# Attention row sums: 15 of 24 steps folded by GpSimd and reduced by VectorE instead of accumulated by ScalarE

## The chip, the cores and the metric

The kernel runs on one core of one Trainium2 chip. The metric is the device time of one execution in microseconds. Before the change it is 11398.82 us, the median of three runs (11398.53 to 11410.69). The profiled execution has a span of 11403.8 us with a mean granted TensorE clock of 0.894.

## What is computed

The reference is a network of four layers on an input of 4 images, 128 channels, 64 by 64. Only the attention of layer 2 is touched. Each image is 4096 tokens with 128 features, that is 16 heads of 8. Queries, keys and values are one and the same matrix:

```python
q = jnp.transpose(qkv, (0, 2, 1, 3))
scores = jnp.einsum('bhsd,bhtd->bhst', q, q) / np.sqrt(D)
attn = jax.nn.softmax(scores, axis=-1)
ctx = jnp.einsum('bhst,bhtd->bhsd', attn, q)
```

As queries and keys are equal, the score matrix is symmetric: a block of exps and its transpose serve both halves. The softmax is taken without a maximum, as exps divided by their sums at the end. A sum for a token has two sources: one from the product of the exps with a column of ones, and one, for transposed blocks, from the row sums of the exps. It is the row sums that the change moves.

## The kernel before

The layer works on one image at a time. For each of the four images `attention` runs once (line 909), between stages that prepare the next image and finish the last. It takes the 16 heads one after another.

**Steps.** The 4096 tokens are four blocks j of 1024 query columns and 16 pairs m of key tiles (256 rows). Because of the symmetry a block j takes only the pairs m from 4j on. Its four own pairs (m // 4 == j) are the diagonal; the later ones are called `behind` and are used twice, straight and transposed. `pairs` (line 962) mixes them: for j=0 three behind and then one own, for j=1 two and one, for j=2 one and one, for j=3 only own. That makes 40 steps for a head, 24 of them behind; steps are counted here from 0 in each head. In order of m they are 4 5 6 0 7 8 9 1 10 11 12 2 13 14 15 3 for j=0 (steps 0 to 15), 8 9 4 10 11 5 12 13 6 14 15 7 for j=1 (16 to 27), 12 8 13 9 14 10 15 11 for j=2 (28 to 35), and 12 to 15 for j=3 (36 to 39).

**What a step does.** TensorE computes scores for two tiles (lines 1082 to 1089) into a ring of three PSUM tiles. ScalarE takes the exps (line 1094), one 128x1024 ACTIVATE for each of the two tiles; in a behind step it also asks for the row sum by `accum_out`, which shows in the trace as an ACTIVATION_READ_ACCUMULATOR after the ACTIVATE. VectorE transposes the exps of behind steps in 32 by 32 blocks (line 1098). One step later `weigh` (line 1026) has TensorE multiply the exps with the values into `ctx_ps`.

**Turns.** The transposed exps of four behind pairs are a group. `turn` (line 980) multiplies one eighth of a group with the spread values `turned_v` into `acc_ps`. After the eighth turn of a group VectorE copies or adds the result into `acc` (lines 1006 and 1008). `turns` (line 1015) does none to three turns in a step and begins a group only two steps after its last transpose. At the end of a block j, `weigh` adds the matching `acc` by the `place` products and VectorE copies `ctx_ps` out (line 1057). TensorE can't start the next block's products before that copy.

**Order.** TensorE follows the source (`manual_schedule` for PE, line 1207): in each step scores, then turns, then the products of the step before. The other engines' order is made by a scheduler when the program is built, and each engine then works through its own in sequence.

**Loads.** `load` (line 921) fetches the keys and queries of a head by 32 small DMAs into a buffer `raw`, and GpSimd rounds `raw` into the fp32r tiles (line 940). `load_values` (line 944) fetches values by four DMAs and has GpSimd spread them by a mask into `turned_v` (line 954).

Of the kernel before, what the change touches and what calls it, by code (L numbers as in the profile page):

```python
# [9 lines left out]
F32 = mybir.dt.float32  # L10
F32R = mybir.dt.float32r
I32 = mybir.dt.int32
AF = mybir.ActivationFunctionType
ALU = mybir.AluOpType
AX = mybir.AxisListType
PSUM = bass.MemoryType.PSUM

P = 128
NB = 4
HW = 64  # L20
L = HW * HW
CH = 512
# [752 lines left out]
def layer2_attention(K, xd, dpool, w):  # L775

    nc, tc, mm = K.nc, K.tc, K.mm
    NH, HD = 16, 8
    NJ = 4
    BT = NTT // NJ  # L780
    scale = 1.0 / math.sqrt(HD)
    with ExitStack() as ctx:
# [126 lines left out]
        def attention(qt, dsum, big, work, pssc, psctx, psacc):  # L909
# [8 lines left out]
            dacc = big.tile([P, NJ - 1, NH, NTT], F32, name="dacc")  # L918
            nc.gpsimd.memset(dacc, 0.0)

            def load(h, queues=(nc.sync, nc.sync)):

                out = []
                for keys in (True, False):
                    t = work.tile([P, L // 2], F32R, name="keys" if keys else "queries")
                    raw = work.tile([P, L // 2], F32, name="raw")
                    n = P if keys else CH
                    for p in range(2):  # L930
                        for c in range(2):
                            for k in range(4):
                                r = unit(p, c).start + HD * k
                                src = head_d[k // 2 if keys else k % 2, HD * h : HD * h + HD]
                                at = p if keys else c
                                queues[not keys].dma_start(
                                    out=raw[r : r + HD].rearrange("d (m s) -> d m s", s=n),
                                    in_=src.rearrange("d (m z s) -> d m z s", z=2, s=n)[:, :, at],
                                )
                    nc.gpsimd.tensor_copy(t, raw)  # L940
                    out.append(t)
                return out

            def load_values(h, j):


                v = work.tile([P, 4 * BT, HD], F32, name="v")
                for a in range(4):
                    nc.sync.dma_start(
                        out=v[32 * a : 32 * a + 32],  # L950
                        in_=value_d[h, :, j].rearrange("s q t d -> s (q t) d"),
                    )
                t = work.tile([P, 4 * BT, 4, HD], F32, name="turned_v")
                nc.gpsimd.tensor_tensor(  # L954
                    t,
                    v.unsqueeze(2).to_broadcast([P, 4 * BT, 4, HD]),
                    quarter.unsqueeze(1).to_broadcast([P, 4 * BT, 4, HD]),
                    ALU.mult,
                )
                return t  # L960

            def pairs(j):

                later = list(range(4 * j + 4, NTT // 2))
                n = len(later) // 4
                for k in range(4):
                    yield from later[n * k : n * k + n]
                    yield 4 * j + k

            steps = [(h, j, m) for h in range(NH) for j in range(NJ) for m in pairs(j)]  # L970
            heads = {0: load(0, (nc.sync, nc.scalar))}
            values = {(0, 0): load_values(0, 0)}
            order = [(h, j) for h in range(NH) for j in range(NJ - 1)]
            cps = psctx.tile([P, CH], F32, name="ctx_ps")
            aps = psacc.tile([P, 2, BT, 32], F32, name="acc_ps")
# [4 lines left out]
            def turn():  # L980

                r, h, j, i, td, _, sums = groups[0]
                if r == 0:
                    sums = groups[0][-1] = aps[:, halves[0] % 2]
                    halves[0] += 1
                groups[0][0] += 1
                tv = values[h, j]
                for g in range(4):
                    n = 4 * r + g
                    q, t = divmod(n, BT)  # L990
                    at = 32 * (4 * t + q)
                    mm(
                        sums[32 * g : 32 * g + 32],
                        tv[:, n].rearrange("p a d -> p (a d)"),
                        td[:, :, at : at + 32],
                        start=r == 0,
                        stop=r == BT - 1,
                    )
                if r < BT - 1:
                    return False  # L1000
                groups.pop(0)
                if i == 1:
                    accs[h] = work.tile([P, NJ - 1, BT, 32], F32, name="acc")
                at = accs[h][:, i - 1]
                if j == 0:
                    nc.vector.tensor_copy(at, sums)  # L1006
                else:
                    nc.vector.tensor_tensor(at, at, sums, ALU.add)
                if i == NJ - 1:
                    after = order.index((h, j)) + 2  # L1010
                    if after < len(order):
                        values[order[after]] = load_values(*order[after])
                return True

            def turns(n, ready):
# [10 lines left out]
            def weigh(h, j, m, exs):  # L1026

                last = m == 4 * j + 3
                first = m == (4 * j + 4 if j < NJ - 1 else 4 * j)
                for p in range(2):  # L1030
                    at = (h * NTT + 2 * m + p) * (HD + 1)
                    for c in range(2):
                        mm(
                            cps[unit(p, c), :],
                            qt[:, at : at + 32],
                            exs[p][:, c, :],
                            start=first,
                            stop=last and j == 0,
                        )
                if not last:  # L1040
                    return
                if j > 0:
                    while any(g[1] == h and g[3] == j for g in groups):
                        turn()
                    for k in range(2):
                        for p in range(2):
                            for c in range(2):
                                a = 2 * p + k
                                mm(
                                    cps[unit(p, c), :].rearrange("r (t a s) -> r t a s", a=4, s=32)[:, :, a],  # L1050
                                    place[:, a, :],
                                    accs[h][:, j - 1, 4 * c : 4 * c + 4],
                                    start=False,
                                    stop=k == 1,
                                )
                u = work.tile([P, CH], F32, name="ctx")
                nc.vector.tensor_copy(u, cps)  # L1057
                for p in range(2):
                    for c in range(2):
                        cols = slice((2 * j + c) * CH, (2 * j + c + 1) * CH)  # L1060
                        r = unit(p, c).start
                        nc.sync.dma_start(out=num_d[p, HD * h : HD * h + HD, cols], in_=u[r : r + HD])
                        nc.sync.dma_start(out=den_d[p, h : h + 1, cols], in_=u[r + HD : r + HD + 1])

            values[order[1]] = load_values(*order[1])


            starts = [n for n, (h, j, m) in enumerate(steps) if m // 4 > j and m % 4 == 0]
# [1 line left out]
            begun = {}  # L1070
            turned = None
            past = None
            for n, (h, j, m) in enumerate(steps):
                keys, queries = heads[h]
                if n == 0 or h != steps[n - 1][0]:
                    if h + 1 < NH:
                        heads[h + 1] = load(h + 1)
                behind = m // 4 > j
                if n in ends:
                    turned = work.tile([P, BT, 2 * CH], F32, name="turned")  # L1080
                    end = min(ends[n], (h + 1) * len(steps) // NH - 2)
                sps = [pssc.tile([P, 2, CH], F32, name="score") for p in range(2)]
                for p in range(2):
                    for c in range(2):
# [2 lines left out]
                            keys[unit(p, c), m * P : (m + 1) * P],  # L1087
                            queries[unit(p, c), j * CH : (j + 1) * CH],
                        )
                exs = []  # L1090
                for p in range(2):
                    ex = work.tile([P, 2, CH], F32, name="ex", bufs=6)
                    t = 2 * m + p
                    nc.scalar.activation(  # L1094
                        ex, sps[p], AF.Exp, scale=scale, accum_out=dacc[:, j, h, t : t + 1] if behind else None
                    )
                    if behind:
                        nc.vector.transpose(turned[:, t % BT, :], ex.rearrange("p c s -> p (c s)"))  # L1098
                    exs.append(ex)
                turns(n, lambda g: begun[id(g[4])] < n - 1)  # L1100
                if past is not None:
                    weigh(*past)
# [4 lines left out]
            while groups:  # L1107
                turn()
            weigh(*past)
            nc.vector.tensor_reduce(dsum, dacc.rearrange("p j h t -> p t h j"), AX.X, ALU.add)  # L1110

        def feed_forward(b, dsum, work, psum):
# [530 lines left out]
```

## Time and profile before

Groups of instructions in the attention, over the whole execution:

| engine, line | what | count | busy us | mean ns |
|---|---|---|---|---|
| ScalarE L1094 | exp, 128x1024 | 5120 | 5015.9 | 1040 |
| ScalarE L1094 | read of the accumulator | 3072 | 680.4 | 221 |
| VectorE L1098 | transpose, 128x1024 | 3072 | 3596.9 | 1219 |
| TensorE L89 | ctx products | 20480 | 2872.8 | 603 |
| TensorE L89 | turns | 24576 | 1750.8 | 387 |
| TensorE L89 | scores | 10240 | 1365.0 | 500 |
| VectorE L1057 | copy of ctx | 256 | 169.7 | 663 |
| GpSimd L954 | spread values, 128x1024 | 192 | 456.4 | 2378 |
| GpSimd L940 | round keys or queries, 128x2048 | 128 | 242.4 | 1894 |

TensorE's matmuls for four parts of the array run beside each other, so their busy times in the table overlap and don't add up to a time. A row's mean is the time of one instruction; the idle time before a group, and what ended it, stand behind it in the page. What sets the pace is read from the order in time.

### The profile page before, as it was taken

How to read it: one execution, taken by the hardware profiler on the slowest of the kernel's cores; microseconds unless marked ns; L12 is line 12 of the kernel's file. 1: busy time of each engine (PE TensorE's matmuls, PEld its weight loads, DVE VectorE, ACT ScalarE, POOL GpSimd, SP SyncE). 2: the span in 40 equal slices, each digit the busy share in tenths (PEclk: the TensorE clock that was granted, in tenths of full speed). 3: DMA queues.
4: the chain of work that ended last, by engine and by line, in shares of the span. 5: the costliest groups of instructions: out<-in, count | busy, mean ns of one | idle time of the engine just before them, and what ended most of it. 6: DMA issues, size and time to landing. Idle time of an engine off the chain costs nothing. (4 is left out here: it accounts for less than half of the span.)

```text
span 11403.8 us, 182690 instructions
## 1 busy us (share of the span) xinstructions
PE 9270.3 (81%) x71376; PEld 3448.3 (30%) x71376; DVE 7274.7 (64%) x7758; ACT 7509.0 (66%) x11610; POOL 2630.9 (23%) x1711
## 2 busy tenths in 40 slices
PE   5777777777759999958999967999967999976766
PEld 2222223222123333323333322333322333323433
DVE  2687687687736666656666655666655666654464
ACT  2564554554428888848888847888846888852331
POOL 0466455565611111121111121111121111110000
PEclk8888878888679999979999979999979999988898
DMA  3322322322122121122211122122122112112103
GB/s 84 89 63 56 95 61 66 86 63 66 49 57 34 32 32 32 34 66 35 37 31 32 24 74 38 32 33 36 24 71 41 31 31 33 31 55 87 49 16 133
DMA packets 524322, 581.50 MB, mean 51 GB/s; under 512 B 106232, under 2 KB 329536, under 8 KB 520896
## 3 DMA queue, kind: packets, MB, share of 16 engines
q1 hardware_dynamic: 520896, 565.61, 21.6%
q8 instruction: 561, 9.19, 0.3%
q10 hardware_dynamic: 2560, 4.20, 0.3%
q14 instruction: 305, 2.50, 0.1%
HBM read 373.96 MB, written 76.55 MB: 40 GB/s over the span
## 5 line engine op out<-in xcount | busy, mean ns | idle before, releaser
L1094 ACT ACTIVATE ex<-score 128x1024 f32<-128x1024 f32 x5120 | 5015.9, 1040 | 665.4 <-PE score L89 657.3
L1098 DVE STREAM_TRANSPOSE turned<-ex 128x1024 f32<-128x1024 f32 x3072 | 3596.9, 1219 | 1595.6 <-ACT ex L1094 1453.1
L89 PE MATMUL ctx_ps<-ex,qt 128*32 128x512 f32 x20480 | 2872.8, 603 | 230.4 <-DVE ctx L1057 229.7
L89 PE MATMUL acc_ps<-turned,turned_v 128*32 128x256 f32 x24576 | 1750.8, 387 | 99.2 <-DVE acc L1006 49.7
L89 PE MATMUL score<-queries,keys 32*128 32x512 f32 x10240 | 1365.0, 500 | 185.4 <-POOL queries L940 182.1
L641 DVE TENSOR_TENSOR_SCAN hs<-decay,carry,hs 128x512 f32<-128x512 f32 x1024 | 1248.0, 1263 | 151.2 <-ACT decay L640 141.9
L640 ACT ACTIVATE decay<-dt,a_neg 128x512 f32<-128x512 f32 x1024 | 699.9, 690 | 883.0 <-DVE hs L641 879.4
L954 POOL TENSOR_TENSOR turned_v<-v,quarter 128x1024 f32<-128x1024 f32 x192 | 456.4, 2378 | 3549.9 <-PE acc_ps L89 3432.7
L89 PEld LDWEIGHTS score<-queries,keys 32*128 32x128 f32 x10240 | 529.3, 183 | 2262.3 <-issue 1589.0
L647 POOL TENSOR_TENSOR hs<-hs,c_sb 128x1024 f32<-128x1024 f32 x512 | 1201.4, 2367 | 49.1 <-DMA c_sb<-c_d 29.4
L89 PEld LDWEIGHTS ctx_ps<-ex,qt 128*32 128x32 f32 x20480 | 683.1, 110 | 832.8 <-DVE ctx L1057 310.3
L89 PEld LDWEIGHTS acc_ps<-turned,turned_v 128*32 128x32 f32 x24576 | 607.3, 108 | 780.2 <-issue 514.9
L89 PE MATMUL y_ps<-hs,pair 128*64 128x512 f32 x2048 | 658.8, 761 | 224.4 <-POOL hs L647 224.3
L637 DVE TENSOR_TENSOR hs<-dtx,b_ps 128x2048 f32<-128x2048 f32 x256 | 581.5, 2271 | 316.8 <-PE b_ps L89 227.8
L1094 ACT ACTIVATION_READ_ACCUMULATOR ex<-score 128x1 f32 x3072 | 680.4, 221 | 0.0
L89 PE MATMUL ln_var<-ln_sq,mean 128*128 128x512 f32 x448 | 296.3, 748 | 220.5 <-ACT ln_sq L104 185.1
L89 PE MATMUL b_ps<-dbc,spread 32*128 32x512 f32 x512 | 343.8, 756 | 149.6 <-DVE hs L637 149.6
L89 PE MATMUL conv<-under,deep 96*32 96x512 f32 x1536 | 283.2, 715 | 74.4 <-DMA under<-xp 54.6
L89 PEld LDWEIGHTS y_ps<-hs,pair 128*64 128x64 f32 x2048 | 138.3, 161 | 674.2 <-POOL hs L647 418.0
L940 POOL CAST keys<-raw 128x2048 fp32r<-128x2048 f32 x64 | 121.1, 1892 | 917.9 <-DMA raw<-head_d 865.2
L644 POOL COPY carry<-hs 128x4 f32<-128x4 f32 x256 | 64.9, 253 | 1108.9 <-DVE hs L641 1096.0
L1057 DVE COPY ctx<-ctx_ps 128x512 f32<-128x512 f32 x256 | 169.7, 663 | 198.5 <-PE ctx_ps L89 198.5
(340 smaller groups left out, 8583.1 us busy)
## 6 DMA issues: line engine op xcount, KB each, us to landing
raw<-head_d SPq DMA_DIRECT2D x1984, 64.0 KB
c_sb<-c_d SPq DMA_DIRECT2D x512, 128.0 KB
dt<-dt SPq DMA_DIRECT2D x128, 256.0 KB
dtx<-dtx SPq DMA_DIRECT2D x128, 256.0 KB
w<-in_L_ffn_weight SPq DMA_DIRECT2D x32, 1024.0 KB
w<-in_L_ffn_weight SPq DMA_DIRECT2D x128, 256.0 KB
under<-xp SPq DMA_DIRECT2D x384, 66.0 KB
under<-fp SPq DMA_DIRECT2D x384, 66.0 KB
```

The lines of the kernel that those rows point to most:

```text
L89: self.nc.tensor.matmul(out, lhsT, rhs, start=start, stop=stop)
L637: nc.vector.tensor_tensor(hs, dtx2, bb.unsqueeze(1).to_broadcast([P, NQ, CH]), ALU.mult)
L640: nc.scalar.activation(ex, dt2[:, q, :], AF.Exp, scale=a_neg[:, q, g : g + 1])
L641: nc.vector.tensor_tensor_scan(hs[:, q, :], ex, hs[:, q, :], carry[:, g, q : q + 1], ALU.mult, ALU.add)
L644: nc.gpsimd.tensor_copy(carry[:, g, :].unsqueeze(2), hs[:, :, CH - 1 : CH])
L647: nc.gpsimd.tensor_tensor(at, at, cs.unsqueeze(1).to_broadcast([P, 2, CH]), ALU.mult)
L940: nc.gpsimd.tensor_copy(t, raw)
L954: nc.gpsimd.tensor_tensor(t, v.unsqueeze(2).to_broadcast([P, 4 * BT, 4, HD]), quarter.unsqueeze(1).to_broadcast([P, 4 * BT, 4, HD]), ALU.mult,
L1057: nc.vector.tensor_copy(u, cps)
L1094: nc.scalar.activation(ex, sps[p], AF.Exp, scale=scale, accum_out=dacc[:, j, h, t : t + 1] if behind else None)
L1098: nc.vector.transpose(turned[:, t % BT, :], ex.rearrange("p c s -> p (c s)"))
```

## The change

Of the 24 behind steps of a head, 15 no longer ask ScalarE for the row sum. `folded` names them: for j=0 m = 4, 5, 7, 8, 10, 11, 13, 14; for j=1 m = 8, 10, 12, 14; for j=2 m = 12, 13, 14. For these GpSimd adds the two halves of each tile's exps (128x1024 out) and then the halves of that (128x512 out), and VectorE reduces 2 x 256 columns to two sums. The reduce is put into the source two steps later. The aim is to relieve ScalarE by GpSimd, which has much idle time.

To make room for it, the rounding of keys and queries is done in place, without the `raw` buffers, and is put late in the head before (8 and 12 steps ahead of its end). The spreading of values is parted from their load and put three steps after it. The exps of a step become one tile with a ring of four, for single tiles with a ring of six.

```diff
-                    raw = work.tile([P, L // 2], F32, name="raw")
+                    raw = t.bitcast(F32)
...
-                    nc.gpsimd.tensor_copy(t, raw)
...
+            def rounded(t):
+
+                nc.gpsimd.tensor_copy(t, t.bitcast(F32))
...
-                        values[order[after]] = load_values(*order[after])
+                        waiting.append((now[0] + 3, order[after], load_values(*order[after])))
...
+            def folded(j, m):
+
+                return ((m - 4) % 3 < 2, m % 2 == 0, m % 4 < 3)[j]
+
+            def fold(n, exs, at):
+                hs = work.tile([P, 2, CH], F32, name="folded", bufs=3)
+                half = CH // 2
+                nc.gpsimd.tensor_tensor(hs, exs[:, :, 0], exs[:, :, 1], ALU.add)
+                nc.gpsimd.tensor_tensor(hs[:, :, 0:half], hs[:, :, 0:half], hs[:, :, half:], ALU.add)
+                folds.append((n + 2, hs, at))
...
+                    if n % per in (per - 12, per - 8):
+                        rounded(heads[h + 1][n % per == per - 8])
+                while waiting and n >= waiting[0][0]:
+                    _, at, v = waiting.pop(0)
+                    values[at] = spread_values(v)
...
-                exs = []
+                exs = work.tile([P, 2, 2, CH], F32, name="ex", bufs=4)
+                aside = behind and folded(j, m)
                 for p in range(2):
-                    ex = work.tile([P, 2, CH], F32, name="ex", bufs=6)
+                    ex = exs[:, p]
                     t = 2 * m + p
+                    summed = behind and not aside
                     nc.scalar.activation(
-                        ex, sps[p], AF.Exp, scale=scale, accum_out=dacc[:, j, h, t : t + 1] if behind else None
+                        ex, sps[p], AF.Exp, scale=scale, accum_out=dacc[:, j, h, t : t + 1] if summed else None
                     )
                     if behind:
                         nc.vector.transpose(turned[:, t % BT, :], ex.rearrange("p c s -> p (c s)"))
-                    exs.append(ex)
+                if aside:
+                    fold(n, exs, dacc[:, j, h, 2 * m : 2 * m + 2])
+                while folds and folds[0][0] <= n:
+                    _, hs, at = folds.pop(0)
+                    nc.vector.tensor_reduce(at, hs[:, :, 0 : CH // 2], AX.X, ALU.add)
```

More of the change, by code (lines that the diff above doesn't have):

```diff
@@ L952, in load_values, with spread_values @@
                     )
+                return v
+            def spread_values(v):
                 t = work.tile([P, 4 * BT, 4, HD], F32, name="turned_v")
@@ L971, in attention @@
             heads = {0: load(0, (nc.sync, nc.scalar))}
-            values = {(0, 0): load_values(0, 0)}
+            for t in heads[0]:
+                rounded(t)
+            values = {(0, 0): spread_values(load_values(0, 0))}
+            waiting = []
             order = [(h, j) for h in range(NH) for j in range(NJ - 1)]
@@ L1035, in weigh @@
                             qt[:, at : at + 32],
-                            exs[p][:, c, :],
+                            exs[:, p, c, :],
                             start=first,
@@ L1063, in weigh @@
                         nc.sync.dma_start(out=den_d[p, h : h + 1, cols], in_=u[r + HD : r + HD + 1])
-            values[order[1]] = load_values(*order[1])
+            values[order[1]] = spread_values(load_values(*order[1]))
+            folds = []
+            def folded(j, m):
[6 more added lines that the diff above has]
+                folds.append((n + 2, hs, at))
             starts = [n for n, (h, j, m) in enumerate(steps) if m // 4 > j and m % 4 == 0]
@@ L1072, in attention @@
             past = None
+            now = [0]
+            per = len(steps) // NH
             for n, (h, j, m) in enumerate(steps):
+                now[0] = n
                 keys, queries = heads[h]
-                if n == 0 or h != steps[n - 1][0]:
-                    if h + 1 < NH:
+                if h + 1 < NH:
+                    if n % per == 0:
                         heads[h + 1] = load(h + 1)
+                    if n % per in (per - 12, per - 8):
[3 more added lines that the diff above has]
+                    values[at] = spread_values(v)
                 behind = m // 4 > j
@@ L1109, in attention @@
             weigh(*past)
+            assert not folds
             nc.vector.tensor_reduce(dsum, dacc.rearrange("p j h t -> p t h j"), AX.X, ALU.add)
```

## The prediction

> **What bounds the kernel now.** I read four views: the windows of the four attention stretches, the groups, the timeline of one head, and the built order of VectorE before and after. Attention takes 5709 of 11403.8 us; the change touches nothing else.
>
> ```profile
> core 0: us, PE busy (x) PEld busy (x) DVE busy (x) ACT busy (x) POOL busy (x), PEclk, DMA share, GB/s
> 3403.00:4828.00 1425.00, 1341.81 (x14572) 480.21 (x14566) 967.96 (x928) 1269.85 (x2048) 170.12 (x78) 0.99 0.19 31
> sum 5709.00, PE 5376.17 PEld 1922.78 DVE 3871.87 ACT 5081.09 POOL 681.68; mean PE 1344.04 PEld 480.70 DVE 967.97 ACT 1270.27 POOL 170.42
> ```
>
> TensorE is at 94% and ScalarE at 89%, VectorE at 68% and GpSimd at 12%. So GpSimd looks free and ScalarE worth relieving. What an accumulator costs ScalarE stands in the timeline around 4210:
>
> ```profile
> 4209.36 1.02 ACT L1094 ACTIVATE ex<-score 128x1024 f32<-128x1024 f32 x1 [1.43 <-PE score L89]
> 4210.28 0.19 ACT L1094 ACTIVATION_READ_ACCUMULATOR ex<-score 128x1 f32 x1
> 4210.37 1.02 ACT L1094 ACTIVATE ex<-score 128x1024 f32<-128x1024 f32 x1
> 4211.37 2.85 ACT L1094 ACTIVATE ex<-score 128x1024 f32<-128x1024 f32 x3
> ```
>
> With accumulator the exps start 1.00 us apart (4210.37 to 4211.37); the three at 4211.37 without reads take 2.85, so (2.85 - 1.02)/2 = 0.915 apart. The read's 0.2 us mostly overlaps: 0.09 us each is paid, 0.18 per step.
>
> A head is 40 steps and lasts 88.9 us (exps of head 5 start at 3848.2, of head 6 at 3937.1). Steps go at three paces: about 1.99 us where ScalarE sets it with accumulators, 1.81 without, and 2.30 where TensorE has two "turns" of old columns to do. VectorE keeps up in all of them, but without slack:
>
> ```profile
> 3867.27 4.67 DVE L1098 STREAM_TRANSPOSE turned<-ex 128x1024 f32<-128x1024 f32 x4 [1.49 <-ACT ex L1094]
> 3871.86 0.39 DVE L1006 COPY acc<-acc_ps 128x256 f32<-128x256 f32 x1
> ```
>
> ```profile
> 3871.60 0.83 PE L89 MATMUL score<-queries,keys 32*128 32x512 f32 x4
> 3872.36 1.07 PE L89 MATMUL acc_ps<-turned,turned_v 128*32 128x256 f32 x16
> ```
>
> The four transposes (m=10, 11) end at 3871.94, the acc copy at 3872.25, and at 3872.36 TensorE begins the turns that read those transposes. At three later places it already waits for VectorE:
>
> ```profile
> 3883.30 1.07 PE L89 MATMUL acc_ps<-turned,turned_v 128*32 128x256 f32 x16 [0.22 <-DVE acc L1006]
> 3897.05 1.07 PE L89 MATMUL acc_ps<-turned,turned_v 128*32 128x256 f32 x16 [0.56 <-DVE acc L1006]
> 3909.77 0.64 PE L89 MATMUL acc_ps<-turned,turned_v 128*32 128x256 f32 x8 [0.46 <-DVE acc L1008]
> ```
>
> So five times a head (steps 11, 16, 22, 28, 36) a late transpose is a late TensorE, microsecond for microsecond: its order is written by hand, and scores and ctx products are queued behind those turns.
>
> [...] A VectorE instruction waiting for GpSimd thus holds all transposes behind it; the timeline agrees, rows of an engine never overtake. [...] so I charge no lock. The trace agrees for transposes: 1199 to 1249 ns over all 3072, some beside GpSimd. [...]
>
> **The change part by part.** Write T for a step's two transposes, F for its fold (two GpSimd adds), R for its reduce.
>
> Removed: 30 of 48 accumulators a head, 15 steps by 0.18 = 2.6 us of ScalarE. It counts only where ScalarE sets the pace: folded steps 4, 5, 19, 25, 30, 32 run at 1.99; the other nine are bound by TensorE (2.30) or sit beside a ctx copy. Six by 0.18 = 1.06 us a head, 68 us in 64 heads. Steps 4 and 5 then lose theirs again to the transposes ahead of the turns at step 6 (T of m=7 ends at 13.1 us either way), leaving some 45.
>
> Added: F is a 128x1024 add, 2.37 us (hs row), plus a 128x512 add, 1.29 (rows of 1265 to 1311 ns), plus some 0.1 for waits: 3.75. Bounds 3.55 (the 1184 ns row, no waits) and 3.95. R reads 128x512: one such row shows 667 ns, another 128x128 takes 259; I take 0.62, bounds 0.5 and 0.75. T lasts 2.33 from the first exp's end, 2.28 back to back. GpSimd's load is 15 x 3.75 + 3 x 2.38 + 2 x 1.89 = 67 us of 89; VectorE's is 24 x 2.3 + 15 x 0.62 + 6 x 0.39 + 4 x 0.66 = 69. Both fit as sums.
>
> Moved, and this decides: the source queues R two steps after its fold, but only TensorE keeps source order. The built VectorE order of a head after the change (numbers are m; C is the ctx copy, A an acc copy or add; | parts groups of four: j=0 up to T15, then j=1 from T8, j=2 from the second T12) is:
>
> ```
> T4 C T5 R4 T6 R5 T7 | T8 T9 R7 R8 T10 R10 T11 A R11
> T12 T13 R13 T14 R14 T15 A | T8 C R8 T9 T10 R10 T11 A
> T12 R12 T13 T14 R14 T15 A | T12 R12 C T13 R13 T14 R14 T15 A C A
> ```
>
> Ten reduces stand directly behind their own step's T (one has C between). F starts when the second exp ends and takes 3.75; T ends 1.2 after that exp. So such an R waits 2.5 us, and the next T starts 3.75 + 0.62 = 4.4 us after the exp that F needed, when it could have started after 2.3.
>
> Stepping through head 5 (us from 3848.2; exp times from its timeline, less 0.09 for a folded second exp):
> - Step 8 to 11: F8 follows F7 and ends 19.05, R8 19.75, T10 22.05 (before 21.47). F10 runs 19.95 to 23.65, R10 ends 24.3, T11 26.6, A 27.0: turns at 27.1 instead of 24.2. **+2.9.**
> - Step 11 to 16: exps move 2.95 later. R13 ends 35.95, T14 38.25; F14 follows F13 and ends 39.05, R14 39.7, T15 42.0, A 42.4: turns at 42.5 instead of 35.1. **+7.4.**
> - Step 16 to 22: T8, C at 45.4, back to +6.4 there; F10 ends 54.75, R10 55.4, T11 57.7, A 58.1: 58.2 instead of 48.9. **+9.3.**
> - Step 22 to 28: rounding keys and spreading values (4.3 us) stand before F12, which ends 62.8; R12 63.45, T13, T14 68.3, F14 70.4, R14 71.05, T15 73.35, A 73.8: 73.9 instead of 61.6. **+12.3.**
> - Step 28 to 36: R12 stands before C, which ends 77.4 instead of 65.4; R13, T14, R14, T15 end 85.35, 87.65, 89.05, 91.35, A 91.75: 91.85 instead of 78.65. **+13.2.**
>
> The sums already hold the exps saved. A head becomes 102.1 us. 64 heads by 13.2 = 845 us: 11399 + 845 = 12244, say 12240.
>
> At no cost: the in-place rounding (same 128x2048 cast, 1.89 us, on GpSimd; the loads go into the buffer that the head before last left, at the head's start, 32 issues, wanted some 50 us later); values split from spreading (same add, waits beside other work); exp buffers of four steps for three (ScalarE waits only for scores here); other stages untouched.
>
> **Rivals.**
> 1. Faster: the waits are hidden, as VectorE has a third of its time free. For it: both load sums fit. Against: turns start 0.1 us after the transposes end. It gives 11399 minus 45 to 166 (ScalarE's ceiling, 64 x 2.6), about 11330.
> 2. Only the ctx copies and half of the reduces bite, the others finding VectorE late anyway or F shorter: +6 a head, 11780.
> 3. A lock slows folds or transposes: 1 us more on each of some eight folds a head that stand in the chain, +8: 12240 + 510 = 12750. Against it: transposes beside GpSimd stay at 1.2 us.
>
> **How the numbers follow.** The stepping gives 12240, chance 0.74. Eight folds and some eight reduces stand in the chain: low bounds take 8 x 0.2 + 8 x 0.12 = 2.6 off a head, 166 us, 12075; high bounds add as much, 12410. Rival 1 has 0.10, rival 2 0.08, rival 3 0.05, something unseen 0.03. The range runs from 11900 to 12480, leaving rivals 1 and 3 out and most of rival 2. Faster 0.10, same 0.02, slower 0.88.
>
> **What would show it.** Right: idle of VectorE before the reduces, ended by GpSimd's fold, some 2 us on ten of fifteen; TensorE waiting for acc copies some 12 us a head; heads near 102 us; fewer accumulator reads, 1152; granted clock lower as TensorE idles. Wrong: reduces with no idle before them (rival 1), folds far from 3.75 or transposes above 1.25 (rival 3), or added TensorE idle in places other than the five.

## The result, and the profile after

The changed kernel takes 12666.48 us, the median of four runs (12649.57 to 12667.91), beside 11398.67 us for the kernel before on the same chip. The ratio is 1.1111, with a 95% interval of 1.1092 to 1.1131. The forecast was 12240 us with a range of 11900 to 12480: the direction was right, the loss is half as large again, and the time lies outside the range.

The first view is the windows of the four attention stretches after (only the first and the sum are shown). Columns are as in the prediction: length, busy time of each engine, then the granted TensorE clock.

```profile
core 0: us, PE busy (x) PEld busy (x) DVE busy (x) ACT busy (x) POOL busy (x), PEclk, DMA share, GB/s
3411.50:5149.60 1738.10, 1439.48 (x14570) 507.08 (x14569) 1121.18 (x1168) 1234.68 (x1568) 1040.23 (x558) 0.91 0.17 25
sum 6956.10, PE 5760.18 PEld 2030.91 DVE 4484.82 ACT 4937.90 POOL 4161.01; mean PE 1440.04 PEld 507.73 DVE 1121.21 ACT 1234.48 POOL 1040.25
```

The stretches grew from 5709.0 to 6956.1 us, 19.5 us for each of the 64 heads, and that is 1247 of the 1268 us lost. Two different things are in it. TensorE stands idle for 6956.1 - 5760.2 = 1195.9 us where it was 332.8: 13.5 us more a head. And for the same matmuls it is busy 5760.2 us where it was 5376.2: 6.0 us more a head, at a clock of 0.91 instead of 0.99. The forecast had the first of these (13.2 us) and not the second.

The groups of the page name the added work and the added wait (busy us and mean ns, then idle before them and what ended it):

```profile
L1126 ACT ACTIVATE ex<-score 128x1024 f32<-128x1024 f32 x5120 | 4916.1, 1029 | 2059.3 <-issue 1214.2
L1130 DVE STREAM_TRANSPOSE turned<-ex 128x1024 f32<-128x1024 f32 x3072 | 3615.5, 1218 | 1028.7 <-ACT ex L1126 844.9
L1084 POOL TENSOR_TENSOR folded<-ex 128x1024 f32<-128x1024 f32 x960 | 2281.7, 2377 | 2200.0 <-ACT ex L1126 2197.9
L89 PE MATMUL acc_ps<-turned,turned_v 128*32 128x256 f32 x24576 | 1913.5, 417 | 1076.1 <-DVE acc L1015 698.7
L1135 DVE TENSOR_REDUCE dacc<-folded 128x2 f32<-128x512 f32 x960 | 651.2, 679 | 1057.3 <-POOL folded L1085 1050.1
L1085 POOL TENSOR_TENSOR folded<-folded 128x512 f32<-128x512 f32 x960 | 1225.9, 1277 | 75.0
```

A fold is 2377 + 1277 ns, a reduce 679 ns, a transpose 1218 ns as before. VectorE stands idle 1050 us ahead of the reduces until GpSimd has folded. The list of waits shows the same idle time handed on to TensorE (us in total, times, longest):

```profile
DVE dacc L1135 <- POOL folded L1085: 1050.1, 658, 3.1
PE acc_ps L89 <- DVE acc L1015: 698.7, 192, 4.6
PE acc_ps L89 <- DVE acc L1017: 348.9, 124, 4.1
```

658 of the 960 reduces wait, 1.6 us each in the mean. The turns wait 1047.6 us for the acc copies where they waited 99.1 (49.7 and 49.4) before, 14.8 us more a head.

One such place in order of time, step 11 of head 5 of the first image, with heads counted from 0 as in the prediction (start, length, engine, line, operation; idle before it and its releaser in brackets):

```profile
3978.97 2.40 POOL L1084 TENSOR_TENSOR folded<-ex 128x1024 f32<-128x1024 f32 x1 [0.85 <-ACT ex L1126]
...
3979.24 1.94 ACT L1126 ACTIVATE ex<-score 128x1024 f32<-128x1024 f32 x2 [0.35 <-issue]
...
3981.44 1.27 POOL L1085 TENSOR_TENSOR folded<-folded 128x512 f32<-128x512 f32 x1
...
3982.75 0.69 DVE L1135 TENSOR_REDUCE dacc<-folded 128x2 f32<-128x512 f32 x1 [1.64 <-POOL folded L1085]
3983.35 2.36 DVE L1130 STREAM_TRANSPOSE turned<-ex 128x1024 f32<-128x1024 f32 x2
3985.64 0.39 DVE L1015 COPY acc<-acc_ps 128x256 f32<-128x256 f32 x1
3986.08 1.19 PE L89 MATMUL acc_ps<-turned,turned_v 128*32 128x256 f32 x16 [2.92 <-DVE acc L1015]
3987.03 1.95 PE L89 MATMUL ctx_ps<-ex,qt 128*32 128x512 f32 x8
3988.91 0.80 PE L89 MATMUL score<-queries,keys 32*128 32x512 f32 x4
3989.64 1.37 PE L89 MATMUL acc_ps<-turned,turned_v 128*32 128x256 f32 x16
3990.84 1.03 PE L89 MATMUL ctx_ps<-ex,qt 128*32 128x512 f32 x8
```

Six of the first seven rows are the forecast's chain: fold, reduce, the last transposes, the copy, then the turns, with TensorE idle for 2.92 us. The other, that of ScalarE, shows that the reduce held up what stood behind it: the exps of the last transposes were done at 3981.18, and VectorE stood idle for 1.64 us until the fold was done at 3982.71, and began these transposes at 3983.35, after the reduce. The last four are what the forecast left out. After that wait the ctx products take 1.95 us for 1.04 and the scores 0.80 for 0.51; the speed is back at 3990.84. The windows of the same stretch show that this is the granted clock (the third number from the end), which is halved for 3.42 us and then full again:

```profile
3983.48:3986.89 3.41, 0.81 (x16) 0.55 (x20) 3.02 (x4) 1.96 (x4) 2.82 (x2) 1.00 0.55 79
3986.89:3990.31 3.42, 3.42 (x28) 0.91 (x20) 2.48 (x3) 0.52 (x1) 0.00 (x0) 0.50 0.09 16
3990.31:3993.72 3.41, 3.41 (x48) 1.23 (x40) 2.37 (x2) 2.76 (x4) 1.91 (x1) 1.00 0.00 0
```

### The profile page after: what moved, and what is told of

Its sections match the earlier page's. It is cut to its first block, busy times and chain, and to the rows that moved or that the text cites. A ratio compares the mean times of both kernels' runs of the same rounds, so it can differ in the third digit from the quotient of the medians.

```text
span 12665.8 us, 182505 instructions
## 1 busy us (share of the span) xinstructions
PE 9672.4 (76%) x71376; PEld 3566.3 (28%) x71376; DVE 7890.8 (62%) x8718; ACT 7365.3 (58%) x9690; POOL 6110.2 (48%) x3631
## 5 line engine op out<-in xcount | busy, mean ns | idle before, releaser
L1126 ACT ACTIVATE ex<-score 128x1024 f32<-128x1024 f32 x5120 | 4916.1, 1029 | 2059.3 <-issue 1214.2
L1130 DVE STREAM_TRANSPOSE turned<-ex 128x1024 f32<-128x1024 f32 x3072 | 3615.5, 1218 | 1028.7 <-ACT ex L1126 844.9
L1084 POOL TENSOR_TENSOR folded<-ex 128x1024 f32<-128x1024 f32 x960 | 2281.7, 2377 | 2200.0 <-ACT ex L1126 2197.9
L89 PE MATMUL ctx_ps<-ex,qt 128*32 128x512 f32 x20480 | 3045.1, 652 | 119.1 <-DVE ctx L1066 118.4
L89 PE MATMUL acc_ps<-turned,turned_v 128*32 128x256 f32 x24576 | 1913.5, 417 | 1076.1 <-DVE acc L1015 698.7
L89 PE MATMUL score<-queries,keys 32*128 32x512 f32 x10240 | 1424.7, 523 | 182.7 <-DMA keys<-head_d 96.6
L1135 DVE TENSOR_REDUCE dacc<-folded 128x2 f32<-128x512 f32 x960 | 651.2, 679 | 1057.3 <-POOL folded L1085 1050.1
L1085 POOL TENSOR_TENSOR folded<-folded 128x512 f32<-128x512 f32 x960 | 1225.9, 1277 | 75.0
L89 PEld LDWEIGHTS score<-queries,keys 32*128 32x128 f32 x10240 | 559.8, 192 | 2428.8 <-issue 1815.1
L89 PEld LDWEIGHTS acc_ps<-turned,turned_v 128*32 128x32 f32 x24576 | 640.3, 114 | 1840.3 <-issue 813.9
```

Of the source, the lines that this page charges most:

```text
L89: self.nc.tensor.matmul(out, lhsT, rhs, start=start, stop=stop)
L1084: nc.gpsimd.tensor_tensor(hs, exs[:, :, 0], exs[:, :, 1], ALU.add)
L1085: nc.gpsimd.tensor_tensor(hs[:, :, 0:half], hs[:, :, 0:half], hs[:, :, half:], ALU.add)
L1126: nc.scalar.activation(ex, sps[p], AF.Exp, scale=scale, accum_out=dacc[:, j, h, t : t + 1] if summed else None)
L1135: nc.vector.tensor_reduce(at, hs[:, :, 0 : CH // 2], AX.X, ALU.add)
```

## The experiments

**Theory A**: the loss comes from where the reduces stand in VectorE's order (they wait for folds, transposes wait behind them, TensorE behind those), plus the slow spell that follows each wait. **Rival B**: the loss comes from the folds, reduces and rounding as work, wherever they stand. Below, a step's time is the distance of its first exp to the next step's, the mean over heads 1 to 14 (of 0 to 15) of all four images.

**The order alone.** The same instructions, but VectorE in the order of the source, in which a reduce stands two steps after its fold; then the opposite, every reduce directly behind its own step's transposes.

```diff
-                    tc.manual_schedule(engines={mybir.EngineType.PE}),
+                    tc.manual_schedule(engines={mybir.EngineType.PE, mybir.EngineType.DVE}),
```
```diff
 # e2_reduce_at_once has this besides
-                folds.append((n + 2, hs, at))
+                folds.append((n, hs, at))
```

> The changed kernel with VectorE too kept in source order, so each reduce stands behind the transposes of two steps later; the folds, loads and buffers are the same. Theory A (the reduce's place holds the transposes up): the five waits of TensorE vanish and the saved accumulators count; 11330 to 11480 us, TensorE's granted clock back near 0.89. Rival B (GpSimd's fold chain, or exp buffers held by folds, is the bound): 12500 or more, as the folds are unchanged. Rival C (the added VectorE work of 15 x 0.68 us a head is paid in full): 11399 + 650 = about 12050.

> As the run before it, but with the reduce put into the source in the step of its own fold, so that all 15 stand directly behind their own transposes. Theory A: five waits again, and the reduce of step 0 now stands before a ctx copy too (3 to 4 us more in each of 64 heads); 12700 to 13000 us. Rivals B and C: the place of the reduce does not matter, so the same time as with the reduce two steps later.

Measured: 11614.81 us in source order, ratio 1.0195 (1.018 to 1.021), clock 0.894; 13152.25 us with the reduces at once, ratio 1.154 (1.1522 to 1.1557), clock 0.851. The two kernels differ in the place of the reduces alone, and that moves the time by 1540 us; the scheduler's order lies between. So 82% of the loss (0.1111 - 0.0195 of 0.1111) hangs on VectorE's order (the first edit orders all of its instructions, not the reduces alone), and B falls as the main cause. But 11615 is above what A expected (11330 to 11480). The waits of the kernel in source order, and VectorE and TensorE around step 16 of one head, show why:

```profile
PE acc_ps L89 <- DVE acc L1015: 274.4, 184, 2.4
PE acc_ps L89 <- DVE acc L1017: 144.3, 124, 1.9
```

```profile
3992.17 4.70 DVE L1130 STREAM_TRANSPOSE turned<-ex 128x1024 f32<-128x1024 f32 x4
3996.79 0.65 DVE L1135 TENSOR_REDUCE dacc<-folded 128x2 f32<-128x512 f32 x1
3998.31 0.69 DVE L1135 TENSOR_REDUCE dacc<-folded 128x2 f32<-128x512 f32 x1 [0.88 <-POOL folded L1085]
3998.92 0.41 DVE L1015 COPY acc<-acc_ps 128x256 f32<-128x256 f32 x1
...
3999.39 1.07 PE L89 MATMUL acc_ps<-turned,turned_v 128*32 128x256 f32 x16 [2.34 <-DVE acc L1015]
```

Two steps are too short a lag. The source has the reduces ahead of the turns, so two of them, one of them waiting for its fold, stand between the last transpose and the acc copy. Step 16 is 2.97 us longer than before (1.0 comes back at step 17), steps 11, 22, 28 and 36 by 0.6 to 0.9 each. The 2.34 us here were followed by turns at full speed (1.07). That is not so everywhere: in 32 of the 64 heads the products behind this wait are slow, and 0.82 of the 2.97 us comes after the turns.

**Without folds, and with folds out of the way.** e3 keeps all of the change but the folding: the 24 row sums are ScalarE's again. e7 queues the reduces a step later and behind the step's turns. e8 does so with six folded steps only, and e11 with four.

```diff
 # e3_no_fold, in the changed kernel
-                aside = behind and folded(j, m)
+                aside = False
```
```diff
 # e7_after_turns, in e1_source_order
-                folds.append((n + 2, hs, at))
+                folds.append((n + 3, hs, at))
...
-                while folds and folds[0][0] <= n:
-                    _, hs, at = folds.pop(0)
-                    nc.vector.tensor_reduce(at, hs[:, :, 0 : CH // 2], AX.X, ALU.add)
                 turns(n, lambda g: begun[id(g[4])] < n - 1)
                 if past is not None:
                     weigh(*past)
+                while folds and folds[0][0] <= n:
+                    _, hs, at = folds.pop(0)
+                    nc.vector.tensor_reduce(at, hs[:, :, 0 : CH // 2], AX.X, ALU.add)
```
```diff
 # e8_six_after_turns and e11_four_after_turns, in e7_after_turns
-                return ((m - 4) % 3 < 2, m % 2 == 0, m % 4 < 3)[j]
+                return (m in (7, 8), m in (10, 14), m in (13, 14))[j]   # e8
+                return (False, m in (10, 14), m in (13, 14))[j]         # e11
```

> The changed kernel without folding: all 24 behind steps ask ScalarE for the row sum again; rounding in place, values spread late and the exp ring of four steps stay. If these parts cost nothing, as predicted: 11399 within 0.3%. Rival D (in-place rounding or late values make a head wait for its keys or values): 11480 us or more.

> VectorE in source order, all 15 folds, but each reduce put three steps after its fold and behind the turns and the ctx products of that step, so that acc and ctx copies come first. Theory A: the 225 us left when the reduces stood two steps later were reduces in front of acc copies (steps 11, 16, 22, 28); they go, and what the accumulators give is left: 11340 to 11400 us. Rival C (VectorE's added 10 us a head are the cost): still 11500 or more.

> The same with six folds a head instead of 15 (m = 7, 8; 10, 14; 13, 14), those where ScalarE set the pace before. If the step times of the kernel before tell which accumulators matter: as fast as 15 folds or faster, 11330 to 11390 us. If all 15 accumulators matter: slower than 15 folds by 9/15 of what those gain over the kernel before.

> Changed kernel with only four folded steps (m=10, 14 of the second group of columns, m=13, 14 of the third), VectorE in source order, reduces queued three steps after the fold and behind that step's turns: e8_six_after_turns without its two folds in the first group. There the step that lost was step 11 (0.59 us a head, one reduce ahead of the transposes), and the saved steps 4 and 5 were given back at step 6. Theory A (folding pays only where ScalarE sets the pace and VectorE has slack): the loss at step 11 goes, the 0.16 us each at steps 19 and 25 and 0.08 each at 30 and 32 remain less 0.2 at steps 22 and 28, so 0.3 us a head below before: 11365 to 11390, at or under e3_no_fold. Rival (any reduce on VectorE costs what its fold saves): 11395 to 11415.

| kernel | us (median) | ratio to before, 95% | sum of step changes, us a head |
|---|---|---|---|
| no folds (e3) | 11388.16 | 0.9988 (0.9982 to 0.9995) | -0.38 |
| 15 folds, reduces after turns (e7) | 11441.26 | 1.003 (1.0019 to 1.004) | +0.21 |
| 6 folds, the same (e8) | 11415.41 | 1.0009 (1.0 to 1.0017) | -0.15 |
| 4 folds, the same (e11) | 11379.61 | 0.9986 (0.9979 to 0.9992) | -0.41 |

The rest of the change, the in-place rounding, the parted spreading and the ring of exps, costs nothing and gains 0.1%. In e3's trace TensorE stands idle as long as before (0.02 us a head less); fewer are the slow products after the ctx copy at a head's start, in 5 of 60 heads where it was 25. Why they are fewer was not tested. With the reduces out of the way the folds no longer cost much, but they don't gain either. In e7 the reduces no longer wait for folds (2.1 us in all, the last number of the group's row), but the turns still wait a little, as its list of waits shows:

```profile
PE acc_ps L89 <- DVE acc L1015: 147.9, 192, 1.2
PE acc_ps L89 <- DVE acc L1017: 90.0, 124, 1.1
```
```profile
L1138 DVE TENSOR_REDUCE dacc<-folded 128x2 f32<-128x512 f32 x960 | 624.0, 650 | 2.1 <-POOL folded L1085 2.1
```

This is a reduce's own 0.65 us, on an engine without slack: e7 loses 0.55 at step 11, 0.51 at 16 and 0.67 at 22 and 28, and gets back 1.5 at the ctx copies of steps 17 and 29. On the other side stands all that relieving ScalarE is worth: in e8, 0.18 at steps 4 and 5 (given back as 0.34 at step 6), 0.17 at 19 and 25, 0.08 at 30 and 0.09 at 32. e11 keeps the last four alone; there most of the 0.51 us saved is paid for at steps 1, 22 and 28 (0.15, 0.15 and 0.12), and its time can't be told from that of e3, with no folds. So that e11 fell into the range expected of it says nothing for the folds. e11 and e3 are both slightly faster than the kernel before; that is the rest of the change, not the folding. e7 and e8 came out 20 to 40 us above what was expected: the expectations charged VectorE's reduces too little.

**The slow spell.** Lengths in the trace of the changed kernel say what happens after a wait: for some us a turn's matmul takes 634 ns for 379, a ctx product 1061 for 592, a score 789 for 497. Is this a price of the wait itself? Here a wait of known length was put into the kernel before (VectorE in source order): the last transpose of step 11 is done again two or four times. No fold or GpSimd work comes in, and the source order shows no cost of its own: outside steps 11 and 12 no step of the kernel with four is more than 0.15 us from before.

```diff
                         nc.vector.transpose(turned[:, t % BT, :], ex.rearrange("p c s -> p (c s)"))
+                        if j == 0 and m == 11 and p == 1:
+                            for _ in range(4):        # e4: 2
+                                nc.vector.transpose(turned[:, t % BT, :], ex.rearrange("p c s -> p (c s)"))
```

> The kernel before, with VectorE in source order and the last transpose of the m=11 step of j=0 done three times instead of once (the same result). The turns of step 11 start 2 x 1.15 = 2.3 us later, TensorE idle for some 2.4 us once a head. If a wait costs only itself: 11399 + 64 x 2.3 = 11546 us. If TensorE is also slowed for some us after a wait of this length: 11600 or more.

> The same with the transpose done five times: turns 4.6 us later, TensorE idle for 4.7 us once a head. If a wait costs only itself: 11399 + 64 x 4.6 = 11693 us. If TensorE is slowed to about half after such a wait for 3 to 5 us: 1.5 us or more on top in each head, 11790 us or more, with matmuls of 1.06 us for 0.59 after the wait and a lower granted clock.

Measured: 11624.24 us for two (1.0199, 1.0182 to 1.0216) and 11866.36 for four (1.0413, 1.0398 to 1.0429). That is above the bare length of the transposes in both cases, as theory A had it. In the timeline of the kernel with four, TensorE waits 4.98 us and is then slow:

```profile
3921.40 1.94 PE L89 MATMUL acc_ps<-turned,turned_v 128*32 128x256 f32 x16 [4.98 <-DVE acc L1006]
3923.11 1.94 PE L89 MATMUL ctx_ps<-ex,qt 128*32 128x512 f32 x8
...
3926.83 1.03 PE L89 MATMUL ctx_ps<-ex,qt 128*32 128x512 f32 x8
```

If standing still is the cause, work in the wait must cure it. Four kernels put extra matmuls into that wait, ahead of the turns, into a spare score tile that nothing reads: score products in e9 (16) and e10 (30), which use 32 rows of the array each (32*128 in the rows below) and are issued to two of the four row groups; ctx products in e12 and e14, which use 128 rows and 32 columns each (128*32) and are issued to all four column groups. The 16 calls of e14 leave 32 records in its trace, the 36 of e12 leave 72.

```diff
 # e9_late4_busy (8) and e10_late4_busy15 (15), in e5_late4
+                fill = 15 if n % (len(steps) // NH) == 11 else 0
+                if fill:
+                    spare = pssc.tile([P, 2, CH], F32, name="score")
+                    for k in range(fill):
+                        for c in range(2):
+                            mm(spare[:, c, :], keys[unit(0, c), m * P : (m + 1) * P],
+                               queries[unit(0, c), j * CH : (j + 1) * CH])
```
```diff
 # e12_late4_full (9) and e14_late4_fit (4), in e5_late4
+                if n % (len(steps) // NH) == 11:
+                    spare = pssc.tile([P, 2, CH], F32, name="score")
+                    oh, oj, om, oexs = past
+                    for k in range(4):
+                        for p in range(2):
+                            at = (oh * NTT + 2 * om + p) * (HD + 1)
+                            for c in range(2):
+                                mm(spare[unit(p, c), 0, :], qt[:, at : at + 32], oexs[p][:, c, :])
```

> The kernel before with the transpose of m=11 done five times (11866 us), and in the wait that this makes TensorE is given sixteen matmuls of scores once more, into a buffer that nobody reads. If the time over 64 x 4.6 us is a clock lost to idleness: the wait costs only itself, 11690 to 11740 us, and matmuls after the wait take 0.59 us again. If it is something else in the order: 11866 us or more.

> The kernel before with VectorE in source order, four repeated transposes in the first group's step 11 as in e5_late4, and 30 extra score matmuls (15 pairs, into a spare score tile that nothing reads) ahead of the turns of that step, twice as many as in e9_late4_busy. At the 0.14 us each that they took there they last 4.2 us, of the 4.6 that the transposes make TensorE wait, so that it idles under 0.6 us in one piece. Theory A (a wait costs its own length, and then a spell of half speed because TensorE stood idle): the turns that follow run at full speed, 1.07 us for 16, and the time is 11690 to 11740, 4.6 us a head above before. Rival (the spell does not come from standing idle, or the extra time is VectorE's and not the clock's): the turns again take some 1.9 us, and the time is 11840 or more, as in e5_late4.

> The kernel before with VectorE in source order and four repeated transposes in the first group's step 11, as in e5_late4, and 36 extra matmuls ahead of the turns of that step, in a spare score tile that nothing reads. In e10_late4_busy15 the extra matmuls were of the score's form (two of the four groups of 32 rows of the array at a time), and TensorE fell to half speed in the middle of them, 2 us after they began, without a pause. Here they are of the ctx form (128 rows, all four groups of 32 columns at once), four in 0.455 us, so 4.1 us in all, of the 4.98 that TensorE waits. Theory C (what keeps the speed is use of the whole array, not an occupied queue): the turns run at 1.07 us for 16 and the ctx products at 0.59 each, clock 0.89 or more, and the time is 11690 to 11740. Rival (the spell comes from the late transposes whatever TensorE does meanwhile, for instance from its operands): the turns again take 1.9 us and the time is 11800 to 11870.

> e12_late4_full with its extra matmuls cut to fit the wait. There each of the 36 calls left two records, so they lasted 7.75 us instead of 4.1 and held the turns up themselves by 3.3 us; but the speed stayed full (turns 1.05, ctx products 1.04). Here 16 calls of the same form, 32 records, 3.6 us by the rate traced there, inside the 4.98 us that TensorE waits at that step, leaving 0.5 and 0.8 us idle. Theory C (use of the whole array keeps the speed): turns 1.07, ctx products 1.04, and 11690 to 11740, so less than e5_late4, which waits equally long and does less. Rival: in e12_late4_full the speed came back during the extra 3.3 us, and here the turns are slow: 11800 to 11870.

| kernel | us (median) | ratio, 95% | steps 11 and 12, us above before |
|---|---|---|---|
| four late transposes, no filler (e5) | 11866.36 | 1.0413 (1.0398 to 1.0429) | 7.03 |
| + 16 score products (e9) | 11856.98 | 1.0395 (1.0381 to 1.0409) | 7.13 |
| + 30 score products (e10) | 11808.50 | 1.0364 (1.035 to 1.0379) | 6.32 |
| + 32 records of ctx products (e14) | 11734.72 | 1.0291 (1.0273 to 1.0308) | 5.05 |
| + 72 records of ctx products (e12) | 11950.59 | 1.0485 (1.0467 to 1.0503) | 8.30 |

e9 settled nothing: its fillers lasted 2.23 us, half of the wait, 2.25 us of standing remained, and the turns were slow again. e10 fills the wait to its end. Its timeline in two heads, the first of which stayed fast:

```profile
3806.38 3.70 PE L89 MATMUL score<-queries,keys 32*128 32x512 f32 x30 [0.50 <-ACT ex L1094]
3810.86 1.07 PE L89 MATMUL acc_ps<-turned,turned_v 128*32 128x256 f32 x16 [0.78 <-DVE acc L1006]
...
3900.29 5.08 PE L89 MATMUL score<-queries,keys 32*128 32x512 f32 x30 [0.50 <-ACT ex L1094]
3905.30 1.94 PE L89 MATMUL acc_ps<-turned,turned_v 128*32 128x256 f32 x16
3907.01 1.93 PE L89 MATMUL ctx_ps<-ex,qt 128*32 128x512 f32 x8
```

In 31 of the 64 heads the 30 fillers last 3.70 us; in 33 they fall to half speed 1.7 to 2.7 us after they began, in the middle of uninterrupted work, and the turns behind them are slow though TensorE had not stood still. So an occupied TensorE is not enough. With products that fill the array the spell is gone:

```profile
3895.91 3.64 PE L89 MATMUL score<-ex,qt 128*32 128x512 f32 x32 [0.50 <-ACT ex L1094]
3900.39 1.07 PE L89 MATMUL acc_ps<-turned,turned_v 128*32 128x256 f32 x16 [0.83 <-DVE acc L1006]
3901.28 1.04 PE L89 MATMUL ctx_ps<-ex,qt 128*32 128x512 f32 x8
```

Not one of e14's 24576 turn matmuls takes over 500 ns, where 1264 of e5's do, and it is some 130 us faster than e5 for doing more work. Its turns come 5.05 us later than before, as e5's do, and nothing is lost after them, where e5 loses 1.81 us in step 11 and 0.17 in step 12. e12 missed its number for a plain reason, its fillers being twice as long as meant (7.75 us, which held up the turns), but it too kept the speed, at the highest clock of all (0.898).

The clock records show when the speed falls. In all fourteen traces every change of the clock falls on a grid of 3.413 us, which runs on without regard to heads and steps; of the 302 spells of half clock in the changed kernel's attention 251 last one such window and 51 two. What comes before a spell is read from the work in the window before it. Take for each window of the attention the share of its time that whole-array products fill (turns, ctx and place products, not scores). Over all fourteen traces (heads 1 to 15 of each image) the clock was full in 21962 windows. In 20695 of these the share was 40% or more, and the clock was never halved in the next. In the other 1267 it was less, and the clock was halved in the next 1124 times. Of such windows with a low share the kernel before has 25, all followed by half clock, and the changed kernel 317, of which 283 are. Score products may count too, which was not tried apart: 45 of the 143 exceptions are in e10. The 40% is an estimate read off these counts; no run was made to find it.

So a wait shorter than a window can be enough, and by these counts it matters how much of one window it takes. From the end of the last whole-array product to the start of the next, the changed kernel's attention has 196 gaps of 4.0 to 5.25 us, all followed by slow matmuls, and 64 of 3.5 to 4.0 us, of which 46 are. Of its gaps of 2.25 to 2.5 us, 56 of 60 at the ctx copy of a head's start are followed by slow matmuls, and none of 58 at steps 6 and 36.

## Why the prediction was wrong

**What held.** The bound (TensorE's hand-written order behind VectorE's transposes), the mechanism and the places of the waits; their lengths too, to 0.4 us at four places and 0.7 at step 36. The table takes the stepping of the prediction apart. "Turns later" is the distance from the step's first exp to its turns, after less before; "after the turns" is the same from the turns to the next step's first exp.

| step | predicted, turns later | measured, turns later | measured, after the turns |
|---|---|---|---|
| 11 | 2.9 | 2.99 | +1.00 |
| 16 | 4.5 | 4.11 | +1.95 |
| 22 (from 6.4 after the ctx copy) | 2.9 | 3.10 | +1.59 |
| 28 | 3.0 | 3.10 | +1.63 |
| 36 | 0.9 | 1.62 | +0.21 |

Steps 17 and 29, with the ctx copies, gave back 0.84 and 1.22; the prediction had 1.0 at the first, and had the second in its 0.9 for step 36. Elsewhere the step times moved by under 0.5 us, with at most 0.1 us of it idle TensorE in any sixth place. The signs held as well: 658 waiting reduces of 960, turns waiting 14.8 us more a head for acc copies (some 12 expected), 1152 accumulator reads, a lower clock (0.858, 0.894 before).

**The step that failed** is the sum, from "turns at 27.1 instead of 24.2. +2.9" down to "+13.2". Every wait was charged with its own length, as "a late transpose is a late TensorE, microsecond for microsecond" had it, and work after the wait with its old length. Measured, the waits of steps 16, 22 and 28 are followed by matmuls at about half speed in every head, and that of step 11 in 46 of 64. The last column sums to 6.4 us a head, 64 x 6.4 = 408 us, which is nearly all of the 422 between 12244 and the measured 12666. The waits themselves sum to 14.9 less 2.1, 12.9 us, beside 13.2. The prediction even listed "granted clock lower as TensorE idles" as a sign, and gave it no price, though the trace of the kernel before holds 25 spells of half clock in the attention, each one window of 3.413 us. That the spell is a price of the wait is shown by e5 against e14 (1.98 us a head lost after the turns against none), for a wait of the same length in the kernel before. That it makes up the changed kernel's missing 6.4 us is read from that kernel's own trace, where the clock is halved in those places, and wasn't tried by filling its waits.

**Smaller terms.** A reduce is 0.679 us, not 0.62, inside its bounds of 0.5 to 0.75. A fold is 2.38 + 1.28 + some 0.1, 3.74 in the timeline above: 3.75 was right. The saved accumulators came to 0.18 each at steps 4 and 5, given back at step 6 (0.44) as the prediction said, and 0.14, 0.14, 0.09 and 0.12 at steps 19, 25, 30 and 32: 0.49 us or 31 us in 64 heads, where "some 45" stood. The claims "at no cost" held: e3 has them all and is not slower. Slips in the working change nothing: 15 by 0.18 is 2.7, not 2.6, six by 0.18 is 1.08, and in the lines shown the turns start 0.4 us after the transposes, 0.1 after the acc copy.

**The rivals.** Rival 1 and rival 2 are out. Rival 3, at 12750, is nearest in time and wrong in cause: no lock showed, transposes being 1218 ns (1219 before) and the big fold adds 2343 to 2414 ns throughout. That the folds and reduces would meet none was an assumption: the transposes alone had been measured for it. The range failed because its upper end was built from the bounds of the fold and the reduce alone; a term that was left out of the sum was left out of the range too.

## What to carry to other kernels

An engine with a third of its time free can still have none at the moments that count: look at what stands behind the new instruction in that engine's queue, and let a consumer of another engine's result stand behind everything that is due before that result arrives. When a change makes TensorE wait, allow for a slow spell after the wait: here it cost 1 to 2 us in four places of five, and it followed 56 of 60 gaps of 2.25 to 2.5 us at one place, though none of 58 at two others. A wait that can't be removed was cheaper here when it was filled with matmuls that use the whole array (11735 us in e14, 11866 in e5). And check first what the relief is worth: here ScalarE's saving was about half a us in a head of 89, before any cost.

## What was not expected of the hardware

In these runs TensorE's clock went with the share of the last window of 3.413 us that whole-array products took, not with whether its queue was busy: 30 score products back to back, on two of the four row groups, dropped from 384 to 623 ns each in 33 of 64 heads, while all 2048 extra ctx products of e14 took 592 to 618 ns. The two forms also differ in their operands and in how many run beside each other, and these weren't parted. A share of under 40% of a window was followed by half clock in 1124 of 1267 cases, and the kernel before pays this too: 25 of its 60 waits for the ctx copy at a head's start, 2.25 to 2.5 us without a whole-array product, are followed by slow products.
